# Turning a normalized activation: VectorE blocks of 32 by 32 and plain transfers, in place of DMA transposes of 16-bit planes

## Chip, core, metric

The kernel runs on one core of a Trainium2 chip. A core has TensorE (PE for matmuls, PEld for the loading of weights), VectorE (DVE), ScalarE (ACT), GpSimd (POOL) and SyncE (SP), which here only issues transfers. Sixteen DMA engines serve all queues of the core. The metric is the device time of one execution in microseconds (us); for the kernel before it is 2822.73 us, the median of three runs (2817.69 to 2825.91).

## The reference

A pre-norm graph attention block over 32 graphs of 512 nodes with 512 features. Each graph is one batch. All arithmetic is float32.

```python
h = jnp.maximum(_layernorm(x, axis=-1), 0.0)          # per node, no weights
h = elu(gat_layer(h, mask, W1, a_src1, a_dst1, b1, concat=True))    # 4 heads x 256
h = gat_layer(h, mask, W2, a_src2, a_dst2, b2, concat=False)        # 1 head x 512
x = x + h

def gat_layer(x, mask, W, a_src, a_dst, bias, concat):
    xl = (x @ W).reshape(B, N, H, F)
    asrc, adst = (xl * a_src).sum(-1), (xl * a_dst).sum(-1)
    e = leaky_relu(asrc[:, :, None] + adst[:, None, :], 0.2)
    attn = softmax(where(mask, e, -1e9), axis=1)
    out = einsum("bsdh,bshf->bdhf", attn, xl)         # + bias
```

What the change touches is the very first product, `x @ W` of layer 1. TensorE contracts over partitions, so the normalized x, which has nodes on partitions after its load, must be turned until it has features on partitions. That turned array is `ht`.

## The kernel before, in words

**Stages.** Every batch goes through: load of x and layer norm; turn into `ht` ([128, 4, 512]: feature k*128 + p on partition p, node along the free dimension); projection 1 (`project1`, in two halves of two heads each); masked softmax for four heads (`Soft.first`, `Soft.second`); gathering with the attention weights (`gather1`) and ELU; projection 2; a softmax for one head; gathering (`gather2`) plus the residual; store. The large products are done with seven half-size products each instead of eight, so ahead of each of them VectorE forms sums and differences of blocks (`sums`, `sums1`, `sums2`). For projection 1 these are sums of blocks of `ht`, put into the tile `hs`.

**Order.** The loop over i works on several batches at once: gathering 1 of batch i+1, projection 1 of batch i+2, gathering 2 of batch i-1, projection 2 of batch i+1, and at its end load and norm of batch i+3. The order of the matmuls is the order in which this loop writes them down. The order on every other engine is not: each operation is noted as a job with a cost, with the keys that it reads and writes, and `Program.order` plans all of them with a model of engines and of the two DMA queues, searches over priorities, and emits every engine's instructions in the planned order. In `dma(size, reads, writes, to, at, cost)` the size is the modelled time on the wires and the cost the time to issue.

**The turn before.** `load(b)` brings x in four tiles of 128 nodes into the four slots `x`. `norm(b)` takes mean and variance of each tile on VectorE, and the power -0.5 on GpSimd. `norm_turn(b, t)` normalizes and applies the ReLU in place on ACT, tile by tile. For the first two batches TensorE then turns the tile. For the 30 others a DMA transpose does[...]: ACT copies the float32 tile as 16-bit words into a slot of `adj`, low halves and high halves in separate planes; SP issues a DMA transpose of the planes back into the x slot; ACT copies the planes together again into `ht`. Each tile goes its own way, so ACT, DMA and ACT overlap over the four tiles.

**Shared buffers.** There are four x slots and two adj slots. `sums2` borrows two x slots (t1, t2) for gathering 2 of a batch, and the load of batch i+3 comes after it in the program, so the loads into these two slots wait until gathering 2 has read them. `masks` loads the adjacency through the adj slots. `ht` exists once: it can be written again when both halves of projection 1 have read it.

**Names.** L476, L479, L482, L487 and L493 are the helpers through which all ACT, VectorE, SP-DMA, GpSimd-DMA and TensorE jobs are emitted; L696 is the DMA transpose of the x planes, L637 that of the mask. So in the profile a group is known by its tiles: `adj<-x` is the split into planes, `x<-adj` the DMA transpose, `ht<-x` the joining, `hs<-ht` the first sum of blocks, `mm<-w_sb,ht` and `mm<-w_sb,hs` products of projection 1 (those with 257 columns and hs belong to projection 2).

## Time and profile before

| what | value |
|---|---|
| time, median of 3 runs | 2822.73 us |
| span of the profiled run, granted TensorE clock | 2824.6 us, 0.994 |
| idle of ACT that `p<-dm` transfers ended (largest of ACT) | 100.6 us |
| DMA: bytes, packets, packets under 512 B | 501.96 MB, 373831, 220788 |
| hardware queue q1 (issued by SP), share of 16 engines | 332.67 MB, 42.3% |
| software queue q0 (issued by GpSimd) | 166.74 MB, 25.3% |
| x normalized (`x<-x,stats`), 128 tiles | 101.8 us on ACT, 803 ns each |

A group's row gives line, engine, operation, tiles and shapes, the count, then busy time and mean duration, then the idle time of the engine ahead of it with what ended it. Consecutive instructions of an engine overlap at their ends, so the step from start to start is somewhat shorter than the duration. In a list of waits the columns are the total, the number and the longest wait in us. A wait for several things is put down to the last. SPq is SP's issuing of transfers: its duration is that of the issue, not of the transfer.

### The profile page before, as it was taken

The numbers are of one execution on the slowest core, as the hardware profiler recorded it, in microseconds if no ns is written. First come the engines' busy times: TensorE is split into PE (matmuls) and PEld (weight loads), VectorE is DVE, ScalarE is ACT, GpSimd is POOL, SyncE is SP. The second block draws the span as 40 slices with busy tenths as digits, with TensorE's granted clock in tenths as the row PEclk, the third lists the DMA queues.
The fourth block names the chain that finished last, engine by engine and source line by source line (L and its number), as shares of the span: only waits on it lengthen the run. The fifth ranks groups of instructions, "written<-read, shape, count | busy, mean of one in ns | idle before, by whom it ended". The sixth has DMA issues, their size and how long they took to land.

```text
span 2824.6 us, 39689 instructions
## 1 busy us (share of the span) xinstructions
PE 2763.9 (98%) x12524; PEld 2376.7 (84%) x12524; DVE 2432.9 (86%) x5526; ACT 2381.3 (84%) x4506; POOL 328.3 (12%) x356
## 2 busy tenths in 40 slices
PE   8899999999999999999999999999999999999998
PEld 6588888888888888888888888888888888888876
DVE  7788988898988888888889888888888898898885
ACT  5798888889889889888898888888888888888973
POOL 0100111110111111111101111011111011110110
PEclk9999999999999999999999999999999999999999
DMA  7575866666866666766668766687756776766763
GB/s 220 141 172 149 207 184 171 177 179 184 207 173 171 175 180 186 186 184 171 171 175 203 185 168 178 180 184 186 181 157 183 175 194 185 176 178 176 187 168 101
DMA packets 373831, 501.96 MB, mean 178 GB/s; under 512 B 220788, under 2 KB 225652, under 8 KB 373620
## 3 DMA queue, kind: packets, MB, share of 16 engines
q1 hardware_dynamic: 327828, 332.67, 42.3%
q0 software_dynamic: 45792, 166.74, 25.3%
q8 instruction: 99, 1.62, 0.2%
q14 instruction: 112, 0.92, 0.1%
HBM read 316.41 MB, written 51.31 MB: 130 GB/s over the span
## 4 chain that ended last, share of the span: by engine, by line
PE 49%; DMA 4%; ACT 3%; DVE 2%; issue 1%; ACTq 0%; DVEq 0%; POOLq 0%
PE mm L493 49%; DMA p<-dm 2%; ACT l L476 1%; DMA x<-adj 1%; DMA drr<-flip 1%; DVE p L479 1%; ACT p L476 0%; DMA rr<-drr 0%; ACT ht L476 0%; DVE hs L479 0%; DVE t L479 0%; ACT adj L476 0%; ACT xl L476 0%; ACT x L476 0%; ACT mm L476 0%
## 5 line engine op out<-in xcount | busy, mean ns | idle before, releaser
L493 PE MATMUL mm<-w_sb,hs 128*128 128x257 f32 (+2 forms) x3032 | 698.7, 381 | 15.7 <-DVE hs L479 10.7
L493 PEld LDWEIGHTS mm<-w_sb,hs 128*128 128x128 f32 x3032 | 573.5, 190 | 106.7 <-DVE hs L479 15.0
L487 POOL DMA_DIRECT2D p<-dm x314 | 275.1, 880 | 2336.4 <-DVE p L479 1053.9
L479 DVE CUSTOM_DVE_ANT_1 l<-l,mt 128x512 f32<-128x512 f32 x640 | 424.9, 685 | 131.2 <-ACT l L476 124.9
L476 ACT ACTIVATE p<-p,z 128x512 f32<-128x512 f32 (+1 forms) x636 | 433.4, 711 | 122.2 <-DMA p<-dm 100.6
L493 PE MATMUL mm<-w_sb,ht 128*128 128x258 f32 x2112 | 502.0, 382 | 5.2 <-DVE xl L479 2.1
L493 PE MATMUL mm<-p,xl 128*128 128x256 f32 (+1 forms) x1984 | 478.6, 384 | 1.9 <-ACT xr L476 0.8
L479 DVE SCALAR_TENSOR_TENSOR p<-rr,z 128x512 f32<-128x512 f32 (+1 forms) x636 | 454.0, 740 | 30.8 <-DMA rr<-drr 28.2
L476 ACT ACTIVATE l<-l,low 128x512 f32<-128x512 f32 x640 | 454.5, 712 | 20.5 <-DVE low L479 19.8
L476 ACT ACTIVATE l<-as,z 128x512 f32<-128x512 f32 x640 | 434.8, 711 | 37.7 <-DMA as<-das 36.8
L493 PE MATMUL mm<-w_sb,h 128*128 128x257 f32 x2048 | 459.0, 381 | 5.3 <-ACT mm L476 4.1
L493 PEld LDWEIGHTS mm<-w_sb,ht 128*128 128x128 f32 x2112 | 401.7, 190 | 65.0 <-DVE xl L479 3.2
L493 PEld LDWEIGHTS mm<-w_sb,h 128*128 128x128 f32 x2048 | 389.5, 190 | 65.3 <-ACT mm L476 5.3
L493 PEld LDWEIGHTS mm<-p,xl 128*128 128x128 f32 x1984 | 378.6, 191 | 63.0 <-issue 6.5
L493 PE MATMUL mm<-xl,p 128*128 128x256 f32 (+1 forms) x1024 | 249.2, 386 | 4.4 <-DVE t L479 2.3
L476 ACT ACTIVATE xl<-mm 128x514 f32<-128x514 f32 (+2 forms) x380 | 222.2, 585 | 35.9 <-PE mm L493 33.8
L493 PE MATMUL mm<-t,hs 128*128 128x256 f32 x992 | 234.2, 382 | 7.3 <-ACT mm L476 6.3
L493 PEld LDWEIGHTS mm<-xl,p 128*128 128x128 f32 x1024 | 193.1, 189 | 40.5 <-issue 5.8
L493 PEld LDWEIGHTS mm<-t,hs 128*128 128x128 f32 x992 | 188.0, 191 | 37.6 <-ACT mm L476 9.6
L476 ACT ACTIVATE xr<-h,b_sb 128x512 f32<-128x512 f32 x248 | 171.8, 714 | 24.4 <-DVE h L479 20.4
L479 DVE SCALAR_TENSOR_TENSOR h<-h,b_sb,xr 128x512 f32<-128x512 f32 x248 | 181.9, 744 | 9.9 <-ACT xr L476 9.5
L476 ACT ACTIVATE h<-mm 128x512 f32<-128x512 f32 (+1 forms) x256 | 146.4, 572 | 30.1 <-PE mm L493 29.5
(110 smaller groups left out, 3206.9 us busy)
## 6 DMA issues: line engine op xcount, KB each, us to landing
p<-dm POOLq DMA_DIRECT2D x314, 512.0 KB, 5.6
rr<-drr SPq DMA_DIRECT2D x159, 512.0 KB
x<-in_x_dram SPq DMA_DIRECT2D x128, 256.0 KB
adj<-in_adj_dram SPq DMA_DIRECT2D x128, 256.0 KB
as<-das SPq DMA_DIRECT2D x64, 512.0 KB
t<-in_x_dram SPq DMA_DIRECT2D x62, 512.0 KB
out_dram<-t SPq DMA_DIRECT2D x60, 512.0 KB
dm<-m SPq DMA_DIRECT2D x64, 256.0 KB
```

What stands on the lines that cost most here:

```text
L476: prog.add("ACT", cost, reads, writes, lambda: nc.scalar.activation(*a, **k))
L479: prog.add("DVE", cost, reads, writes, lambda: f(*a, **k))
L487: lambda: nc.gpsimd.dma_start(to, at, accum_op=OP.add), size,
L493: f(*a, **k)
```

## The change

The 16-bit planes and the DMA transposes of x go. For batches from the third on:

- The x slots become slices of one tile `xt4`, and a tile of 128 nodes is loaded into a quadrant of 32 partitions, four nodes' rows to a partition (`"(t r) f -> r t f"`). So slot t holds rows that are 32 partitions' worth of each of the four tiles.
- After the ReLU of all four tiles, `turn(b)` runs four VectorE transposes of 128x512 float32, one for each group of 128 features. Each turns blocks of 32 by 32 within a quadrant of partitions. The first two groups go to the two adj slots, the other two back into the lower half of the x slots.
- 32 plain transfers of 32 KB then bring the blocks from quadrant i to quadrant j of `ht`, sixteen for each half c of the features.
- Keys of x and ht are made finer to match: four quadrants for each x slot, and four pieces j for each (t, c) of ht.

It is meant to take the two casts of each tile off ACT and to do away with transposes in packets of 256 bytes, for four instructions on VectorE and plain transfers.

```diff
     def load(b):
-            dma(1.1, (), [xk], xt, x[b, t * P : (t + 1) * P, :])
+        XT[b] = sorted(((k, t) for k, t in (xs.take() for _ in range(NT))), key=lambda kt: kt[0])
+        for t, (xk, xt) in enumerate(XT[b]):
...
+                dma(
+                    1.1, (), [xk + (t,) for xk, _ in XT[b]], xt4[t * Q : (t + 1) * Q],
+                    x[b, t * P : (t + 1) * P, :].rearrange("(t r) f -> r t f", t=NT),
+                )
...
-            act(
-                0.96, [xk], [ak], words.rearrange("p (h f) -> p h f", h=2),
-                hn.bitcast(U16).rearrange("p (f h) -> p h f", h=2), AF.Copy,
-            )
-            prog.add(
-                "SP", 1.3, [ak], [xk],
-                lambda: nc.sync.dma_start_transpose(
-                    back.rearrange("p (g n) -> p g n", n=P), words
-                ),
-                1.9,
-            )
-            act(
-                1.21, [xk], [("ht", t, 0), ("ht", t, 1)],
-                ht[:, :, t * P : (t + 1) * P].bitcast(U16).rearrange("p k (n h) -> p h k n", h=2),
-                back.rearrange("p (h k n) -> p h k n", h=2, n=P), AF.Copy,
-            )
...
+    def turn(b):
+        every = [q for xk, _ in XT[b] for q in x_keys(xk)]
+        ks = [adjs.take()[0] for _ in range(2)]
+        flat = adj2.bitcast(F32).rearrange("p a n -> p (a n)")
+        low = xt4[:, :, : D // 2]
+        for k in range(KT):
+            c, kk = divmod(k, KQ)
+            into = xt4[:, :, k * P : (k + 1) * P].rearrange("p t (j f) -> p j t f", f=Q)
+            if c == 0:
+                to, keys = flat[:, kk * N : (kk + 1) * N], [ks[kk]]
+                reads, keys = every, [*keys, ("low", kk)]
+            else:
+                to = low[:, 2 * kk : 2 * kk + 2, :]
+                reads, keys = [*every, ("low", 0), ("low", 1)], [("turned", kk)]
+            dve(0.59, reads, keys, nc.vector.transpose, to, into)
+        for c in range(2):
+            for i in range(NT):
+                for j in range(NT):
+                    at = slice(i * Q, (i + 1) * Q)
...
+                    dma(
+                        0.2, keys, [("ht", i, c, j)],
+                        ht[j * Q : (j + 1) * Q, c * KQ : (c + 1) * KQ, i * P : (i + 1) * P], came,
+                        0.35,
+                    )
...
-        return half_blocks(ht, KQ, lambda r, c: [("ht", 2 * r, c), ("ht", 2 * r + 1, c)])
+        return half_blocks(ht, KQ, lambda r, c: ht_keys(2 * r, c) + ht_keys(2 * r + 1, c))
```

More of the change, by code (lines that the diff above doesn't have):

```diff
@@ L430, in tile_gat @@
     hs = sbuf.tile([P, 3, KH, N // 2], F32, name="hs")
-    xs = slots("x", NT, [P, D])
+    xt4 = sbuf.tile([P, NT, D], F32, name="x")
+    xs = Slots("x", [xt4[:, t, :] for t in range(NT)])
     adj2 = sbuf.tile([P, 2, N], I32, name="adj2")
@@ L558, in weights2 @@
             dma(
-                1.5, [("ht", 0, 0)], [("w2", ix)], w2_sb[:, ix, :, :M],
+                1.5, ht_keys(0, 0), [("w2", ix)], w2_sb[:, ix, :, :M],
                 w2[r * HF // 2 : (r + 1) * HF // 2, c * DO // 2 : (c + 1) * DO // 2].rearrange(
@@ L600, in tile_gat, with x_keys, ht_keys @@
     XT, MASK, MASKT, ST = {}, {}, {}, {}
-    def load(b):
-        XT[b] = []
-        for t in range(NT):
-            xk, xt = xs.take()
-            dma(1.1, (), [xk], xt, x[b, t * P : (t + 1) * P, :])
-            XT[b].append((xk, xt))
+    Q = P // NT
+    def x_keys(k):
+        return [k + (i,) for i in range(NT)]
+    def ht_keys(t, c):
+        return [("ht", t, c, j) for j in range(NT)]
+    def load(b):
+        XT[b] = sorted(((k, t) for k, t in (xs.take() for _ in range(NT))), key=lambda kt: kt[0])
+        for t, (xk, xt) in enumerate(XT[b]):
+            if b < 2:
+                dma(1.1, (), x_keys(xk), xt, x[b, t * P : (t + 1) * P, :])
+            else:
[3 more added lines that the diff above has]
+                )
     def masks(b):
@@ L648, in norm @@
         for t, (xk, xt) in enumerate(XT[b]):
-            dve(0.61, [xk], [sk + (t,)], nc.vector.bn_stats, st[:, t, :S], xt)
+            dve(0.61, x_keys(xk), [sk + (t,)], nc.vector.bn_stats, st[:, t, :S], xt)
             dve(TINY, [sk + (t,)], [sk + (t,)], nc.vector.bn_aggr, st[:, t, S : S + A], st[:, t, :S])
@@ L668, in norm_turn @@
         S, A = nc.vector.BN_STATS_DIM, nc.vector.BN_AGGR_DIM
+        keys = x_keys(xk)
         act(
-            0.71, [xk, sk + (t,)], [xk], hn, hn, AF.Relu,
+            0.71, [*keys, sk + (t,)], keys, hn, hn, AF.Relu,
             bias=st[:, t, S : S + 1], scale=st[:, t, S + A : S + A + 1],
@@ L675, in norm_turn @@
             pe(
-                [xk], [pk], 0.44,
+                keys, [pk], 0.44,
                 [(nc.tensor.transpose, (pt[:, k * P : (k + 1) * P], hn[:, k * P : (k + 1) * P], identf), {})
@@ L680, in norm_turn @@
             act(
-                0.62, [pk], [("ht", t, 0), ("ht", t, 1)], ht[:, :, t * P : (t + 1) * P],
+                0.62, [pk], ht_keys(t, 0) + ht_keys(t, 1), ht[:, :, t * P : (t + 1) * P],
                 pt.rearrange("p (k n) -> p k n", n=P), AF.Copy,
@@ L684, in norm_turn @@
             banks.give(pk)
-        else:
-            ak, a = adjs.take()
-            words = a.bitcast(U16)
-            act(
-                0.96, [xk], [ak], words.rearrange("p (h f) -> p h f", h=2),
-                hn.bitcast(U16).rearrange("p (f h) -> p h f", h=2), AF.Copy,
-            )
-            back = hn.bitcast(U16)
-            prog.add(
-                "SP", 1.3, [ak], [xk],
-                lambda: nc.sync.dma_start_transpose(
-                    back.rearrange("p (g n) -> p g n", n=P), words
-                ),
-                1.9,
-            )
-            act(
-                1.21, [xk], [("ht", t, 0), ("ht", t, 1)],
-                ht[:, :, t * P : (t + 1) * P].bitcast(U16).rearrange("p k (n h) -> p h k n", h=2),
-                back.rearrange("p (h k n) -> p h k n", h=2, n=P), AF.Copy,
-            )
-            adjs.give(ak)
@@ L707, in norm_turn @@
-        xs.give(xk)
+            xs.give(xk)
         if t == NT - 1:
             stats.give(sk)
+            if b > 1:
+                turn(b)
+    def turn(b):
[9 more added lines that the diff above has]
+                reads, keys = every, [*keys, ("low", kk)]
+            else:
+                to = low[:, 2 * kk : 2 * kk + 2, :]
[5 more added lines that the diff above has]
+                    at = slice(i * Q, (i + 1) * Q)
+                    if c == 0:
+                        came, keys = flat.rearrange("p (k j n) -> p j k n", k=KQ, j=NT)[at, j], ks
+                    else:
+                        came = low[at].rearrange("p (k u) (v n) -> p u v k n", u=2, v=2)[:, j // 2, j % 2]
+                        keys = [("turned", 0), ("turned", 1), *every]
+                    dma(
[3 more added lines that the diff above has]
+                    )
+        for k in ks:
+            adjs.give(k)
+        for xk, _ in XT[b]:
+            xs.give(xk)
@@ L1007, in project1_first @@
                     pe(
-                        [("ht", t, 0), ("ht", t, 1)]
+                        ht_keys(t, 0) + ht_keys(t, 1)
                         + [q for r in range(2) for k in range(KQ)
@@ L1299, in sums2 @@
         t1, t2 = (
-            (t.rearrange("p (k f) -> p k f", f=M), [k]) for k, t in (xs.take() for _ in range(2))
+            (t.rearrange("p (k f) -> p k f", f=M), x_keys(k)) for k, t in (xs.take() for _ in range(2))
         )
@@ L1342, in gather2 @@
         for n in (5, 6):
-            xs.give(right[n][1][0])
+            xs.give(right[n][1][0][:2])
     def gather2_plain(b, soft):
@@ L1399, in tile_gat @@
     S1, S2 = {}, {}
-    HT_KEYS = [("ht", t, c) for t in range(NT) for c in range(2)]
+    HT_KEYS = [q for t in range(NT) for c in range(2) for q in ht_keys(t, c)]
     for q in range(2):
```

## The prediction, made before the changed kernel ran

> **What bounds the kernel now.** I read the busy line of the page first, then three stretches of the span by the stretches view.

> ```profile
> PE 2763.9 (98%) x12524; PEld 2376.7 (84%) x12524; DVE 2432.9 (86%) x5526; ACT 2381.3 (84%) x4506; POOL 328.3 (12%) x356
> ```

> The stretches are the start, the regular iterations and the end:

> ```profile
> 0.00:130.00 130.00, 107.55 (x383) 75.24 (x384) 101.28 (x342) 82.28 (x165) 13.96 (x19) 0.91 0.68 185
> 130.00:2700.00 2570.00, 2545.08 (x11679) 2215.03 (x11678) 2248.81 (x5008) 2236.88 (x4212) 305.11 (x327) 1.00 0.69 180
> 2700.00:2824.60 124.60, 111.29 (x465) 86.44 (x464) 82.80 (x179) 62.15 (x131) 9.26 (x11) 1.00 0.46 132
> ```

> The columns are the stretch in us, its length, the busy time of PE, PEld, DVE, ACT and POOL, the granted clock, the DMA share and GB/s. In the 2570 us that hold the regular iterations TensorE stands still for 25 us in all. The change adds or removes no matmul, so it can win only from those 25, plus a little at the start; it can lose without a bound. The waits of PE in that stretch say who owns the 25 (total, times, longest):

> ```profile
> PE mm L493 <- DVE hs L479: 10.2, 8, 2.2
> PE mm L493 <- ACT mm L476: 9.4, 12, 1.7
> PE mm L493 <- ACT xl L476: 2.8, 3, 1.2
> PE mm L493 <- DVE t L479: 0.9, 2, 0.7
> PE mm L493 <- DVE xl L479: 0.9, 1, 0.9
> PE mm L493 <- ACT p L476: 0.6, 1, 0.6
> ```

> Two owners matter. ACT ends 9.4 + 2.8 + 0.6 = 12.8 us of waits, mostly PSUM copies that come late on a busy ACT. The eight waits on hs are projection 1 waiting for sums of ht, the end of the chain that is changed: x loaded, normalized, turned, summed. One batch of that chain, by the timeline (start, duration):

> ```profile
> 1052.70 0.34 SPq L482 DMA_DIRECT2D x<-in_x_dram  x1
> ...
> 1066.76 6.26 SPq L696 DMA_TRANSPOSE x<-adj  x2
> ...
> 1083.14 1.23 SPq L696 DMA_TRANSPOSE x<-adj  x1
> ...
> 1091.75 0.69 DVE L479 TENSOR_TENSOR hs<-ht 128x512 f32<-128x512 f32 x1
> ...
> 1093.33 1.90 PE L493 MATMUL mm<-w_sb,hs 128*128 128x258 f32 x8
> ```

> The first line is the last x load; it goes out as soon as the second layer has done with the x slots it borrowed. The last line is the product that needs the first sum. Between them lie 40.6 us, and the order of matmuls fixes that window. The sum begins 1.6 us before its product, so the whole window is used.

> [...] after the 2.2 us wait near 1179 us, the stretch from 1182 to 1185 has clock 0.50.

> **The change, part by part.** It concerns 30 batches (the third to the last).

> *ACT loses two casts a tile.*

> ```profile
> L476 ACT ACTIVATE ht<-x 128x1024 uint16<-128x1024 uint16 x120 | 160.6, 1351 | 1.2 <-DMA x<-adj 1.2
> L476 ACT ACTIVATE adj<-x 128x1024 uint16<-128x1024 uint16 x120 | 125.2, 1046 | 6.1 <-DMA x<-adj 6.1
> ```

> 160.6 + 125.2 = 285.8 us, 9.5 us a batch. ACT in the regular stretch falls from 2237/2570 = 87% to about 76%. If waiting goes as share/(1 - share), it falls from 6.7 to 3.2, so about half of ACT's 12.8 us: **-6.6 us**. The rule is my choice; the ends are 0 and -12.8.

> *VectorE gains four turns of 128x512 a batch.* Nearest row: TENSOR_TENSOR of this size, 684 ns. 120 x 0.69 = 83 us; if fp32 ran at half rate, 120 x 1.22 = 146 us (1219 ns is the row of 128x1024). I take 0.69[...]. DVE goes from 2249/2570 = 87.5% to 90.7%, share/(1 - share) from 7.0 to 9.8: 40% more of the 1.8 us that PE waits for t and xl, **+0.7 us**. At the upper price it would stand at 93% and cost about +2 us.

> *SP loses four transposes and gains 32 plain issues a batch.* A transpose holds the queue 1.27 us (median of 120), 5.1 us a batch. A plain issue takes 333 ns (x loads), 396 ns (t loads, one dimension more) or 524 ns (the flip stores). I take 0.40 with the queue's own step: 32 x 0.40 = 12.8 us, range 11 to 17. SP thus issues some 8 us longer in 87 us, on a queue that mostly waits now. It is in order, so behind the burst stand the rr and as loads of the softmax; the planner knows a price of 0.35 and orders around it.

> *The wires.* The burst moves 1 MB; the page's hardware queue moves 332.67 MB in 42.3% of 2824.6 us, 278 GB/s while all engines work, so 3.8 us a batch[...]. That lies under the issue time. [...] Beside a DMA share of 0.69 I put the net at nothing: the issue time of the burst covers it.

> *The chain.* Loads now write 32 partitions of all four slots, so all four, not the last two, wait for the borrowed slots, and each row statistic waits for all four. Counted from 1052.7, with nothing in the way: loads 5.4 us (1.8 from issue to first statistic in this trace[...]); four statistics 4 x (0.68 + 0.17) = 3.4; power and shift 4.2 as in the trace (last aggregate 1057.30, first possible ReLU 1061.5); four ReLUs 4 x 0.80 = 3.2; two turns 1.4, the others beside transfers; 32 issues 12.8; landing 1.5; first sum 0.7. Sum 32.6 us. Eight other issues now stand in SP between 1072 and 1087; at 0.45 they add 3.6 if all fall inside the burst: 36.2 of 40.6, **4.4 us to spare**. The old chain, counted so: 1.8 + 1.7 + 4.2, four times 0.80 + 1.05, then 1.3 + 1.5 + 1.35 + 0.7 = 20 us; it had 20 to spare, and the trace shows ACT spending it on other work until the end. So a chain with slack on paper came late 8 times in about 30. The new one has less slack, but fewer hand-offs on ACT, which is no longer full. I let a third of the hs waits go: -3.4 us, and -1.1 of the clock loss (two waits over 2 us led to half clock for 3.4 us each, 1.7 lost each): **-4.5 us**. Ends: -13.6, and the rival below.

> *The start.* The first turned batch falls into 100 to 150 us, where PE waits 3.9 us once for a PSUM copy on ACT, with clock lost after it; 9.5 us of casts leave this place: **-1.5 us**, between 0 and -6.

> *At nothing:* finer keys for ht and x (order only), the weights' wait on four keys in place of one, the sorted slots. More DMAs per reader mean more semaphore waits ahead of the first matmul and the sums; one such wait takes 17 to 50 ns[...].

> Sum: -6.6 + 0.7 - 4.5 - 1.5 = -11.9 us, 2822.7 - 11.9 = **2811**.

> **The rivals.**
> - *The burst makes ht late (slower).* The DMAs of this queue signal eight semaphores in turn, and each issue first waits for the one eight earlier. A small transfer lands about 2 us after issue (0.52 plus the mean wait of 51.8/36 = 1.4 us of a load on its das store), so eight in 2 us do not limit; with a 512 KB rr load among them they do, and each such stop eats 1 to 2 us of the 4.4. For it: the waits on hs already lead the list. Against it: SP has room, and the planner puts a tight chain first. With 1 us late in each of 30 batches: +30, less the present 10.2, less 7 for ACT: 2836. With 2 us late, each also paying 1.7 of clock: 60 + 51 - 10 - 7, 2917. Middle of what I expect, not all batches: **2845**.
> - *No change.* The hs waits stay or grow by what ACT saves: -6.6 + 0.7 + 3 gives **2820**. For it: the last in the chain is always as late as the plan lets it be.
> - *Nearly all stalls go.* ACT -11, hs -10, clock -3, start -4: **2795**. Against it: VectorE at 91% replaces ACT as the full engine.

> **How the numbers follow.** Forecast 0.42, nearly all stalls gone 0.08, no change 0.20, late ht 0.30. The band of 0.3% is 8.5 us: below 2814 lie the first two, 0.50; 2820 is within, 0.20; slower 0.30. The range begins at the stalls-gone case, 2795, and goes to 2858, past the late case's middle; left out are the lower half of the 0.08 and somewhat under half of the 0.30. The price of the turn and of an issue (11 to 17 us) act through the chain and lie in it.

> **What would show it.** ACT about 2095 us busy, DVE about 2515; 120 turns of 128x512 near 690 ns; 960 issues into ht near 0.36 to 0.45 us; PE's waits on ACT halved; the chain from last x load to first sum under 41 us in most batches. I am wrong if waits of PE on sums of ht (or on ht itself) pass 20 us, or a half-clock stretch follows them in many batches; if an issue takes 0.5 us or more; or if softmax waits on rr and as grow until PE waits for p.

## The result, and the profile after

The changed kernel takes 3119.08 us (median of four runs, 3111.52 to 3127.54), the kernel before 2820.51 us beside it (2817.69 to 2825.91). The ratio is 1.1057, with a 95% interval of 1.1020 to 1.1094: 299 us more, far outside the range of the prediction.

The first part of the page of the changed kernel, busy time of each engine:

```profile
PE 2854.1 (91%) x12524; PEld 2414.9 (77%) x12524; DVE 2495.7 (80%) x5646; ACT 2139.7 (69%) x4266; POOL 323.9 (10%) x356
```

TensorE runs as many matmuls as before and is busy 90 us longer (2854.1 against 2763.9), for the greater part because of half clock. The record of the granted clock has stretches at 0.50 that make 208 us in this run and 37 us before; TensorE was busy for 159 and 29 us of them, so half clock accounts for about (159 - 29)/2 = 65 us of the 90, an estimate that takes work at 0.50 to last twice as long, as eight matmuls below do (3.78 us against 1.90). The stretches view shows where the rest of the 299 lies (stretch, length, busy time of PE, PEld, DVE, ACT, POOL, clock, DMA share, GB/s):

```profile
0.00:130.00 130.00, 103.39 (x378) 71.85 (x379) 100.93 (x343) 81.32 (x166) 12.36 (x18) 0.99 0.64 177
130.00:3000.00 2870.00, 2642.84 (x11704) 2259.53 (x11703) 2315.05 (x5134) 2001.14 (x3981) 302.22 (x328) 0.97 0.60 161
3000.00:3121.00 121.00, 107.88 (x445) 83.48 (x443) 79.72 (x171) 57.29 (x121) 9.31 (x11) 0.98 0.46 133
```

The start and the end lose little. The loss lies in the regular iterations: PE stands still for 2870.00 - 2642.84 = 227 us there, where it was 25. No engine is full, and the DMA share fell from 0.69 to 0.60, so this is a kernel that waits in line for something. The waits of PE (total, times, longest) say for what:

```profile
PE mm L494 <- DMA ht<-adj: 118.5, 27, 8.4
PE mm L494 <- ACT xl L477: 39.9, 21, 3.8
PE mm L494 <- DVE h L480: 36.4, 21, 6.1
PE mm L494 <- DVE xl L480: 27.2, 17, 3.6
```

Lines of helpers stand one higher than before. The first row is new: TensorE waits for the turned tile itself, 27 times and 4.4 us on average, about once a batch. (The planner placed some of these waits, as the experiments show; the row names only who came last.) The other three do not belong to the turn: xl are the projected nodes, which ACT copies out of PSUM and VectorE combines, and h is the ELU on VectorE. VectorE has its own new wait (total, times, longest), at the sums of ht. In the kernel before, it waited there for no transfer, and 7.5 us for ACT's joining. Here:

```profile
DVE hs L480 <- DMA ht<-adj: 162.9, 42, 7.6
DVE hs L480 <- DMA ht<-x: 61.2, 21, 8.1
```

What the plan put behind these sums on VectorE is late with them. That xl and h are late for this reason is likely, but was not followed instruction by instruction.

One batch by the timeline of SP, the queue that issues all plain transfers (start, duration of issuing, count):

```profile
1732.58 0.81 SPq L483 DMA_DIRECT2D x<-in_x_dram  x2
...
1733.91 0.90 SPq L483 DMA_DIRECT2D x<-in_x_dram  x2
...
1758.38 3.92 SPq L483 DMA_DIRECT2D ht<-adj  x6
1762.41 1.22 SPq L483 DMA_DIRECT2D ht<-x  x2
1763.74 0.56 SPq L483 DMA_DIRECT2D drr<-flip  x1
1764.40 3.79 SPq L483 DMA_DIRECT2D ht<-x  x6
1768.24 7.76 SPq L483 DMA_DIRECT2D ht<-adj  x10
1776.05 0.58 SPq L483 DMA_DIRECT2D rr<-drr  x1
1776.67 6.49 SPq L483 DMA_DIRECT2D ht<-x  x8
1783.27 0.57 SPq L483 DMA_DIRECT2D das<-flip  x1
```

From the first of the 32 transfers at 1758.4 to the end of the last at 1783.2 pass 24.8 us, with two short issues of the softmax between them. The first transfer starts 24 us after the last x load. TensorE in that time, in its own timeline (the bracket holds the idle time and what ended it):

```profile
1769.65 1.89 PE L494 MATMUL mm<-p,xl 128*128 128x256 f32 x8
1779.94 3.78 PE L494 MATMUL mm<-w_sb,ht 128*128 128x258 f32 x8 [8.39 <-DMA ht<-adj]
```

It stands for 8.39 us, until the last transfer of the first half, issued at 1775.4, has landed. Then it pays again: eight matmuls took 3.78 us, where eight of this shape took 1.90 us in the kernel before. The stretches view of those 13 us gives the clock, the third figure from the right of each row:

```profile
1771.00:1780.00 9.00, 0.61 (x4) 0.23 (x2) 1.99 (x4) 1.33 (x2) 0.87 (x1) 0.75 0.51 122
1780.00:1784.00 4.00, 4.00 (x10) 3.12 (x11) 4.00 (x7) 0.85 (x2) 0.00 (x0) 0.50 0.45 135
```

The clock falls to 0.50: its record has 0.50 from 1775.5 us, within the wait of 8.39 us, to 1785.8.

The sizes come from the rows of single instructions (minimum, median and maximum in ns). The issues, from the view of the tile ht:

```profile
L483 SPq DMA_DIRECT2D ht<-adj x480: 585/595/1892, 136.3 to 2933.8; - x160
L483 SPq DMA_DIRECT2D ht<-x x480: 585/595/1962, 143.5 to 2940.7; - x160
```

And the turns, from the view of the tile x:

```profile
L480 DVE STREAM_TRANSPOSE adj<-x x60: 658/700/712, 133.0 to 2916.1; 128x512 f32<-128x512 f32 x60
L480 DVE STREAM_TRANSPOSE x<-x x60: 662/699/712, 138.1 to 2917.5; 128x512 f32<-128x512 f32 x60
```

A turn costs what was forecast. An issue costs 595 ns, 0.64 us from start to start, where the forecast had 0.40 and the plan of the kernel has 0.35. Three causes were open at this point: the 32 issues as such, the plan that was made with a wrong price for them, and the longer way into the turn (quadrant loads of all four slots, VectorE's turns).

### The profile page after: what moved, and what is told of

Read it like the earlier page. It is cut to its first block, busy times and chain, and to the rows that moved or that the text cites. A ratio compares the mean times of both kernels' runs of the same rounds, so it can differ in the third digit from the quotient of the medians.

```text
span 3121.6 us, 40881 instructions
## 1 busy us (share of the span) xinstructions
PE 2854.1 (91%) x12524; PEld 2414.9 (77%) x12524; DVE 2495.7 (80%) x5646; ACT 2139.7 (69%) x4266; POOL 323.9 (10%) x356
## 5 line engine op out<-in xcount | busy, mean ns | idle before, releaser
L494 PE MATMUL mm<-w_sb,hs 128*128 128x257 f32 (+2 forms) x3032 | 720.9, 389 | 47.9 <-DVE h L480 31.8
L494 PEld LDWEIGHTS mm<-w_sb,hs 128*128 128x128 f32 x3032 | 586.6, 195 | 152.0 <-DVE h L480 41.8
L494 PE MATMUL mm<-w_sb,ht 128*128 128x258 f32 x2112 | 550.3, 409 | 152.6 <-DMA ht<-adj 118.5
L494 PEld LDWEIGHTS mm<-w_sb,ht 128*128 128x128 f32 x2112 | 424.4, 204 | 239.5 <-issue 108.9
L494 PE MATMUL mm<-p,xl 128*128 128x256 f32 (+1 forms) x1984 | 485.7, 387 | 11.0 <-ACT p L477 4.7
L480 DVE SCALAR_TENSOR_TENSOR p<-rr,z 128x512 f32<-128x512 f32 (+1 forms) x636 | 451.7, 740 | 32.6 <-DMA rr<-drr 32.4
```

The costliest lines, as they stand in the source:

```text
L480: prog.add("DVE", cost, reads, writes, lambda: f(*a, **k))
L494: f(*a, **k)
```

## The experiments

All times are medians, and all ratios are to the kernel before on the same chip, whose medians were 2820 to 2824 us. The brackets behind a ratio hold its 95% interval. An experiment that starts from the changed kernel says "after".

### Price and number of the issues

**The right price in the plan.** After, with only the price of an issue in the plan changed. The work stays the same, its order is planned anew.

```diff
-                        0.35,
+                        0.64,
```

> The changed kernel; only the planner's price for issuing one of the 32 transfers is put at 0.64 us (0.595 measured, and the step to the next) in place of 0.35. Theory A (the 32 issues themselves, 20.5 us one after the other on SP, lie in the chain from the x load to the sums of ht): no plan shortens them, 3050 to 3130 us. Rival B (a plan made with a wrong price puts the work of all engines into a bad order, and that is most of the loss): under 2950 us.

Measured: 2944.9 us, 1.0407 [1.0360, 1.0455]. One number of the plan takes away 174 of the 299 us. The waits of PE in this run:

```profile
PE mm L494 <- ACT mm L477: 35.7, 23, 4.6
PE mm L494 <- DMA ht<-adj: 28.1, 17, 3.8
```

The wait on the turned tile falls from 118.5 to 28.1 us, while SP issues as many transfers as before. The burst of a batch is no shorter (25.4 us from its first issue to the end of its last, in the median, against 24.2). So the greater part of that first row was not the burst as such. It was the order: not that of the matmuls, which is the same in both kernels, but that of the work of VectorE, ACT and SP around them. It had been planned for a burst of 32 x 0.35 = 11 us, on a queue where it takes 32 x 0.64 = 20.5. VectorE's wait ahead of the sums of ht fell with it, from 224 to 60 us; its larger row is now:

```profile
DVE hs L480 <- DMA ht<-adj: 47.9, 23, 4.1
```

**How far such a result scatters.** The same edit with 0.66 in place of 0.64.

> e1_price with 0.66 us an issue in place of 0.64. The same question for the changed kernel: 2935 to 2955 us if plans with a true price are alike; a wider miss gives the scatter that the smaller differences between these experiments have to be read against.

Measured: 2973.63 us, 1.0516 [1.0474, 1.0557], 29 us above the run with 0.64, and outside what was expected of like plans. The search found another order for this small change of the price, and the two differ by 1%. TensorE's wait on ht<-adj is 61.5 us here, against 28.1, so the part of that row that the order makes scatters too, from 57 to 90 of the 118.5 us. The share of the wrong price is thus 145 to 174 us. This is one pair only, but by it no step of less than about 30 us between two orders of the changed kernel is safe by itself. Does the kernel before scatter as much?

```diff
-                "SP", 1.3, [ak], [xk],
+                "SP", 1.32, [ak], [xk],
```

> The kernel before with the planner's price of the x transpose at 1.32 in place of 1.3, a change that says nothing new to the plan. Measures how far two equally good plans lie apart. If plans are robust: within 6 us of before. If the search scatters: 10 to 30 us off, up or down.

Measured: 2824.05 us, 1.0002 [0.9986, 1.0018], although VectorE has another instruction in 4147 of its 5526 places, ACT in 2816 of 4506. So these two orders of the kernel before are equally good, and the two of the changed kernel are not. That the slack of the chain makes this difference is a reading; the next run shows that the order matters in the kernel before too, once its price is false enough.

**A wrong price in the kernel before.** The same line of the kernel before, with 0.1 in place of 1.3: four transposes of 1.27 us a batch of which the plan knows nearly nothing. No instruction is changed.

> The kernel before, with not one instruction more or less; only the planner is told that a DMA transpose of x takes 0.1 us to issue in place of 1.3, so 4.8 us of SP a batch are unknown to it (the changed kernel hides 32 x 0.29 = 9.3 us). Theory B: a wrong price alone costs tens of us, 2850 to 2980 us. Rival (order hardly matters, the burst's length did it): 2815 to 2840 us.

Measured: 2865.22 us, 1.0167 [1.0120, 1.0215]. A wrong price alone costs 42 us, in a kernel without any of the change. The waits of PE show it where it showed after the change, at the sums of ht, which end the chain of the turn (10.7 us before, over the whole span):

```profile
PE mm L493 <- DVE hs L479: 25.3, 10, 6.4
```

**A quarter of the transfers.** After, with 8 of the 32 transfers of a batch; the others are left out, and so most of ht is not written anew. Once with the price of 0.35, once with 0.64.

```diff
-                for j in range(NT):
+                for j in (i,):
```

> The changed kernel with 8 of the 32 transfers of each batch (those that stay in their own quadrant); the other 24 are left out, so three quarters of ht hold old values. Loads, turns and keys are as in the changed kernel. Theory A: the burst falls from 20.5 to 5.1 us, the chain fits its window of 41 us again, 2795 to 2840 us. Rival C' (the loads into quadrants, or turns that wait for all four tiles, or VectorE's extra work make the loss): over 2980 us.

Measured: 2890.14 us, 1.0226 [1.0190, 1.0262], between the two expectations.

> As e3_quarter (8 of the 32 transfers, the other 24 left out, so three quarters of ht hold old values), but planned at 0.64 us an issue. Theory A+B (burst length in the chain, and the price in the plan): with a burst of 5 us and a true price nothing is left, 2795 to 2835 us. Rival D (loads into quadrants, the turn that waits for all four tiles and VectorE's extra work cost as well): 2870 to 2895 us, as e3_quarter.

Measured: 2854.13 us, 1.0108 [1.0084, 1.0131], again between the two. Against the 32 transfers at the right price (2944.9) this is 91 us less: the length of the burst, 24 issues or 15 us a batch, costs 91 us in 30 batches even when the plan knows it (120 us against the run with 0.66). With the issues their bytes are left out too, so this run does not part the two; a run below moves all the bytes in half as many issues. And the wrong price costs less where there are fewer issues: 36 us with 8 of them, 145 to 174 with 32. PE no longer waits for ht in any row worth showing; its first wait is a PSUM copy on ACT:

```profile
PE mm L494 <- ACT mm L477: 30.1, 22, 3.3
```

### What is left: loads and turns

**Fewer turns.** The run before this, with one of the four turns of a batch; three are left out.

```diff
-            dve(0.59, reads, keys, nc.vector.transpose, to, into)
+            if k == 0:
+                dve(0.59, reads, keys, nc.vector.transpose, to, into)
```

> e5_quarter_price with one of the four VectorE turns of a batch done and three left out (and 24 of 32 transfers left out, so most of ht holds old or unturned values). VectorE gets 2.1 us a batch back. If VectorE's extra work is the 31 us that e5 still lost: 2815 to 2835 us. If not (loads, barrier, or the scatter between plans): 2845 to 2865 us.

Measured: 2828.09 us, 1.0009 [0.9994, 1.0024], the time of the kernel before. Its busy line:

```profile
PE 2761.6 (98%) x12524; PEld 2371.2 (84%) x12524; DVE 2438.0 (86%) x5556; ACT 2129.4 (75%) x4266; POOL 320.1 (11%) x356
```

PE is again as busy as before, and VectorE is within 5 us of before. Two things follow. Three turns fewer a batch go with 26 us less, which is about the scatter of two orders. The traces speak against the chain as the way: in both runs the first sum of ht starts 33.8 us after the borrowed slots come free, and TensorE has matmuls to do until 39.0 us, without a stop (medians of the batches). VectorE's load or the scatter remains. And ACT is 252 us lighter than before, 8 short transfers replace four transposes, the loads still go into quadrants, and yet nothing is won: what the change was for shows no gain here.

**ACT's casts by themselves.** The kernel before, with both casts on a quarter of their columns (the other columns are left out) and priced accordingly.

```diff
-                0.96, [xk], [ak], words.rearrange("p (h f) -> p h f", h=2),
-                hn.bitcast(U16).rearrange("p (f h) -> p h f", h=2), AF.Copy,
+                0.34, [xk], [ak], words.rearrange("p (h f) -> p h f", h=2)[:, :, :P],
+                hn.bitcast(U16).rearrange("p (f h) -> p h f", h=2)[:, :, :P], AF.Copy,
...
-                1.21, [xk], [("ht", t, 0), ("ht", t, 1)],
+                0.4, [xk], [("ht", t, 0), ("ht", t, 1)],
...
```

> The kernel before with both ACT casts of each tile on a quarter of their columns (three quarters left out, so most of ht holds old values), priced accordingly; DMA transposes unchanged. It gives ACT some 6.5 us a batch back and adds nothing anywhere: what the relief of ACT alone is worth. By the prediction's working (half of 12.8 us of waits, and an earlier ht): 2805 to 2815 us. If ACT's load does not matter: within 5 us of before.

Measured: 2823.25 us, 0.9988 [0.9968, 1.0007]. The busy line:

```profile
PE 2761.8 (98%) x12524; PEld 2374.3 (84%) x12524; DVE 2433.9 (86%) x5526; ACT 2212.6 (78%) x4506; POOL 327.3 (12%) x356
```

ACT fell from 2381 to 2213 us, somewhat over half of the casts' 286 us; the time changed by -9 to +2 us, by the interval. So no gain shows, but one of a few us is not ruled out either. The wait of PE on ACT's PSUM copies hardly shrank (13.8 us over the whole span before, 13.0 here).

**Whole slots in place of quadrants.** After, with each x load writing one slot of all partitions. To keep the nodes in order, the turns then write with a step of four elements.

```diff
-                    1.1, (), [xk + (t,) for xk, _ in XT[b]], xt4[t * Q : (t + 1) * Q],
-                    x[b, t * P : (t + 1) * P, :].rearrange("(t r) f -> r t f", t=NT),
+                    1.1, (), x_keys(xk), xt,
+                    x[b].rearrange("(p t) f -> t p f", t=NT)[t],
...
+                to = to.rearrange("p (j n t) -> p j t n", j=NT, t=NT)
...
-                to = low[:, 2 * kk : 2 * kk + 2, :]
+                to = xt4[:, :, kk * P : (kk + 1) * P].rearrange("p j (n t) -> p j t n", t=NT)
...
```

> The changed kernel, but each x load fills one whole slot over 128 partitions (partition p of slot t gets node 4p + t), so the two loads that don't need a borrowed slot go early again[...]; the turns write with a step of four to restore the order of nodes; 32 transfers as before. Theory A with the load as a second term of the same chain: the statistics start about 4 to 5 us sooner, and 28 batches give 110 to 160 us back: 2960 to 3010 us. Rival C (the load doesn't matter, the burst alone sets the time): 3100 to 3130 us.

Measured: 3132.1 us, 1.1082 [1.1042, 1.1123], no gain. The edit brought a cost that nobody expected. The groups of one shape each (busy time, mean of one in ns, idle time before them):

```profile
L480 DVE STREAM_TRANSPOSE x<-x 128x512 f32<-128x512 f32 x60 | 64.3, 1133 | 0.0
L480 DVE STREAM_TRANSPOSE adj<-x 128x512 f32<-128x512 f32 x60 | 63.5, 1129 | 1.2 <-ACT x L477 1.1
```

A turn went from 700 to 1130 ns, and the plan, which has 0.59 for it, did not know. So the time says nothing clear about the loads; the trace says more. Counted from the moment the borrowed slots come free, the last row statistic ends at 6.3 us in the median, where the changed kernel has 12.9. The loads into quadrants do hold up the way in. But the first transfer starts only 2.3 us sooner (20.9 against 23.2), and no time is won by it.

**Half as many transfers, twice as long.** All four turned groups of 128 columns in one row of memory, so that 16 transfers of 64 KB carry them in place of 32 of 32 KB. The loads are the whole slots of the last run, one turned group goes by a slot of adj and a copy on ACT, and an issue is priced 0.64.

```diff
...
-                    dma(
-                        0.2, keys, [("ht", i, c, j)],
-                        ht[j * Q : (j + 1) * Q, c * KQ : (c + 1) * KQ, i * P : (i + 1) * P], came,
-                        0.35,
-                    )
+                dma(
+                    0.4, [*(("turned", k) for k in range(KT)), *every],
+                    [("ht", i, c, j) for c in range(2)],
+                    ht[j * Q : (j + 1) * Q, :, i * P : (i + 1) * P],
+                    xt5[at, j, :].rearrange("p (k n) -> p k n", k=KT),
+                    0.64,
+                )
```

> 16 transfers of 64 KB, each with all four groups of features of a pair of quadrants, in place of 32 of 32 KB; whole-slot loads as in e2; the turned blocks stand in one tile, one group passes through a slot of adj and one ACT copy. Planned at 0.64 us an issue. Theory A: burst 10.3 us, loads 4 to 5 us sooner, so the chain is some 14 us shorter and fits: 2800 to 2850 us. If the issue time grows with the bytes or pieces (1.2 us each), nothing is won over e2: 2960 to 3010 us.

Measured: 2902.59 us, 1.0274 [1.0236, 1.0312], between the two expectations. The issues, from the view of the tile ht:

```profile
L485 SPq DMA_DIRECT2D ht<-x x480: 585/601/2459, 136.5 to 2715.6; - x160
```

An issue of twice the bytes and twice the rows per partition takes 601 ns. So the cost is per issue. The run is 42 us below the one with 32 issues at the right price; the whole-slot loads, the slower turns and the copy on ACT are in this difference too. The turns, again with a step of four, are mispriced here too; with nearly their true price:

```diff
-                0.59, [*every, *(("turned", z) for z in (3, 0, 1, 2)[:q])],
+                1.05, [*every, *(("turned", z) for z in (3, 0, 1, 2)[:q])],
```

> As e4_sixteen, but the turn, which took 1.13 us with its writes of step four, is planned at 1.05 us in place of 0.59. Theory B (a price that the plan doesn't know costs more than the work): 2835 to 2875 us. Rival (the strided turn itself fills VectorE): 2890 to 2910 us, as e4_sixteen.

Measured: 2861.55 us, 1.0131 [1.0099, 1.0164]: another 41 us for a price alone.

**Quadrant loads on the 16 transfers, whole and split.** First the kernel with 16 transfers, loads into quadrants and turns with the unit step again (0.70 us):

> 16 transfers of 64 KB as in e4_sixteen, but loads into quadrants as in the changed kernel, so that the turns write with unit step (0.70 us, planned at 0.59 a step). All prices near the truth. If loads into quadrants are harmless, as e2_slots suggests: 2800 to 2850 us, faster than e4 and e6. If they cost their 4 to 5 us a batch: 2900 us or more.

Measured: 2920.43 us, 1.0338 [1.0311, 1.0365], 59 us more than with whole slots at the right price. Then each quadrant load in two, so that slots 2 and 3, which come free first, are filled first:

```diff
...
+        if b > 1:
+            for u in (2, 0):
+                for t in range(NT):
+                    dma(
+                        0.6, (), [xk + (t,) for xk, _ in XT[b][u : u + 2]],
+                        xt4[t * Q : (t + 1) * Q, u : u + 2],
+                        x[b, t * P : (t + 1) * P, :].rearrange("(t r) f -> r t f", t=NT)[:, u : u + 2],
+                    )
```

> e7_sixteen_quads with each quadrant load cut in two: slots 2 and 3, which nothing borrows, are loaded early, slots 0 and 1 after gathering 2 has done with them (8 loads of 128 KB). Theory C (what loads into quadrants cost is that all four wait for the two borrowed slots, and all statistics for all four loads): e7's excess over e6 and more goes away, 2825 to 2860 us. Rival ([...]the pieces, make them slow): 2900 us or more, as e7.

Measured: 2885.66 us, 1.0230 [1.0185, 1.0276]: 35 of the 59 us come back, less than was expected if the late loads were the cause, more than if not. That looks like a cost of loads which wait for all borrowed slots. But the same split on the kernel with 8 transfers and on that with 32 does not bear it out:

> e5_quarter_price (8 of the 32 transfers, the other 24 left out, so three quarters of ht hold old values; price 0.64) with the loads cut in two as in e9. Theory C: the 31 us that e5 still lost were the late loads, 2805 to 2830 us; if ACT's relief is worth anything, below 2815. Rival (VectorE's turns and the barrier over four tiles): 2845 to 2860 us, as e5.

Measured: 2867.99 us, 1.0175 [1.0132, 1.0217], 14 us more than unsplit.

> The whole changed kernel, all 32 transfers, price 0.64 as in e1_price, and the loads cut in two as in e9. Theory: the late loads cost here what they cost e7, 1.5 to 2 us a batch, so 45 to 60 us come off e1's 2945: 2880 to 2905 us; what then remains over e10 is the burst. Rival (the burst hides the loads): 2935 to 2955 us.

Measured: 2965.46 us, 1.0512 [1.0466, 1.0558], 21 us more than unsplit at 0.64 and 8 us less than unsplit at 0.66. In all three pairs the split brings the last row statistic forward, by 4.0, 1.9 and 3.8 us in the median, and yet the time goes either way. The last two times lie above both of their expectations. Gains and losses here are of the size of the scatter between orders, so what the quadrant loads cost in time stays open. One more cause was not tried: the plan has 1.1 us on the wires for a quadrant load, and no run has another price for it.

**Two queues.** The 16 transfers with split loads, every second one issued by GpSimd.

```diff
...
+                if j % 2:
+                    prog.add(
+                        "POOL", 0.95, keys, [("ht", i, c, j) for c in range(2)],
+                        lambda to=to, came=came: nc.gpsimd.dma_start(to, came), 0.4,
+                    )
+                else:
+                    dma(0.4, keys, [("ht", i, c, j) for c in range(2)], to, came, 0.64)
```

> e9 with every second of the 16 transfers issued by GpSimd (planned at 0.95 us each) in place of SP, so both queues issue side by side. If SP's issue time is what is left: 15 to 30 us less than e9. If the GpSimd queue then holds up its own accumulating transfers into p: slower than e9, with more waits of ACT on p<-dm.

Measured: 2847.92 us, 1.0095 [1.0070, 1.0119], the best full version with turns on VectorE: 38 us less than with all 16 on SP, somewhat more than the scatter of two orders. Its issues, from the view of the tile ht:

```profile
L485 SPq DMA_DIRECT2D ht<-x x240: 585/618/1981, 135.5 to 2650.6; - x120
L742 POOL DMA_DIRECT2D ht<-x x240: 548/556/639, 135.8 to 2649.2; - x120
```

Eight issues a batch on each queue run beside each other, and ht is gone from the first rows of PE's waits. It is still 28 us slower than the kernel before, and no version tried beats that.

## Why the prediction was wrong

Going from after down, step by step: the right price 174 us, 24 transfers fewer 91, three turns fewer 26, and 8 us between that and the kernel before. They add up to the 299. By the run with 0.66 the first two are 145 and 120. The order of the steps is a choice and each has the scatter of an order, about 30 us, in it; the first two are well above that, the third is not.

- **"Nothing to win but 25 us"** was contradicted by no run. The sizes of the turn (700 ns against 0.69), of ACT's relief (2140 us busy against 2095) and of VectorE's load (2496 against 2515) were right. The prediction named the burst as the danger, said that an issue of 0.5 us or more would prove it wrong, and named waits of PE on ht followed by half clock as the sign. All of that is in the trace.
- **"32 issues 12.8 us" is the first step that failed.** It took 0.40, the duration of a t load, which reads from HBM; measured are 0.595 in the row and 0.64 from start to start, 20.5 us. Even the upper end, 17 us, was passed. The nearest row in kind, a store from SBUF, had 0.524 and was used only for that end. With it the sum of the chain would have been 32.6 + 32 x (0.524 - 0.40) + eight foreign issues (3.6) = 40.2 of the 40.6 us of the window, no slack.
- **"The planner knows a price of 0.35 and orders around it" is the second, and the larger.** The prediction counted that as protection. But the plan's 0.35 lies still further below the truth than the prediction's own 0.40, and the prediction saw both numbers and did not ask what a static order does whose price is wrong. It was the largest term of the whole change, 145 to 174 us, and it stood in no sum. The kernel before with a false price, +42 us without any other edit, shows the same by itself.
- **The way in was too short.** "Loads 5.4 us" to the first statistic held 1.8 us from the trace; the rest was the author's estimate, which no trace showed. Counted from the moment the borrowed slots come free, when the first x load is issued, the first statistic starts at 10.1 us in the median of the batches, nearly 5 us late. VectorE stood idle for an x load only four times, 3.8 us in all, so it was its order that put the statistics there. ReLUs ran from 18.6 to 21.5, and the transfers from 23.2 to 47.6 (some 24 us, forecast 12.8 + 3.6). The first sum needs only part of the 32 transfers and starts at 39.8. The first product on ht starts at 43.0, where it was 38.7 in the kernel before; TensorE stands for 4.6 us of that, nearly all of it for ht. This is some 4 of the 10 us by which a batch became longer (96 in place of 86). The other 6 lie behind that product, in waits for xl and h and in matmuls at half clock; how they divide was not settled. What quadrant loads cost in time was not settled either; the run with one turn holds them at no visible cost, and its chain has slack.
- **"VectorE +0.7 us"** was reckoned from VectorE's share of time. Between the runs with four turns and with one lie 26 us, at the edge of the scatter and in a chain that is not late, so neither the size nor the way is shown.
- **"ACT -6.6 us"** cannot be told from nothing: between -9 and +2 us in the kernel before with lighter casts, which does not exclude it, and no gain in the run with one turn. **"hs -4.5 us"** had the wrong sign: the chain now ends at the transfers.
- **The rival "the burst makes ht late"** had the effect, and named a case of 2 us late in every batch, 2917 us. Its size fell short, since its lateness came from stops at semaphores and not from the plain sum of 32 issues with a false price in the plan. In the trace of the changed kernel all 2002 issues of SP behind the first eight signal the semaphore used eight issues before, and 1745 have a recorded wait for it. But SP stopped for it ahead of an issue into ht only three times, 1.7 us in all, 1.0 of it for an rr load. Longer issues are there (85 of 960 took over 700 ns, the longest 1.96 us); what held them was not shown, and what issues take beyond 595 ns makes only 1.9 us a batch.

Where the loss goes in the end: PE stands still 207 us longer than before, summed over the whole span (268 against 61), and is busy 90 us longer, some 65 of them by half clock; that makes 297, the difference of the two profiled runs.

## What to carry to other kernels

Replacing few costly transfers by many cheap ones moved the cost here to the issuing queue: multiply the number of issues by the duration of an issue of the same kind (SBUF to SBUF here, 0.6 us), and compare it with the slack of the chain before anything else. In a kernel whose order is planned from a table of prices, a new operation needs its measured price first, since a false one can cost more than the operation. And look for what the relieved engine was holding up: here TensorE stood at 98%, and the relief of ACT, at 84%, showed no gain.
